# Four edits to the dense part of a four-layer graph network: where ones are counted, where the gate is summed, who adds x, and when fe1 is loaded

## The chip, the cores and the metric

The kernel runs on one core of a Trainium2 chip. The core has a matrix engine (PE), a vector engine (DVE), a scalar engine for activations (ACT), a general engine (GpSimd, POOL in the profile) and a queue for transfers (SP). The metric is the device time of one launch in microseconds, as a median of several runs. A profiled execution is a separate run with a time of its own.

## The reference, cut to what matters

Four layers act on 4096 nodes with 256 features and one adjacency matrix of 4096 x 4096 int32. Each layer normalises x, applies relu, runs a graph block, and adds the result to x. The change concerns the end of layer 0, which has no sum over neighbours left once `h_attn` is known, and the degree of layer 1.

```python
# layer 0, after Wh = h @ W and h_attn = softmax(masked logits) @ Wh
h_enh = silu(_ln(Wh @ fe1_w + fe1_b, fe_ln_g, fe_ln_b)) @ fe2_w + fe2_b
B, C, dt = split(Wh @ W_bcdt + b_bcdt, 3)
hs = Wh * ((softmax(dt + A) * B) @ abp_w + abp_b)
h_part, z = split(hs @ W_hz + b_hz, 2)
hs = (h_part * silu(z) + h_part * D) @ out_w + out_b
hs = hs * (1.0 + C @ cp_w + cp_b)
comb = concatenate([h_attn, hs])
g = sigmoid(silu(_ln(comb @ g1_w + g1_b, g_ln_g, g_ln_b)) @ g2_w + g2_b)
x = x + _ln(g * h_attn + (1.0 - g) * hs + h_enh, ln_g, ln_b)
# layer 1
a = (adj == 1)
deg = sum(a, axis=1)          # needed as 1 / deg for each node
```

## The kernel before, in words

The work is cut into 32 tiles of 128 nodes, and four tiles make a block of 512. The stages follow one another: preparation of layer 0, attention of layer 0, the dense part of layer 0, then layers 1, 2 and 3. A framework schedules the instructions of each engine: it takes the program as Python emits it, works out what depends on what, and fixes an order for each engine and for each transfer queue. Each engine then works strictly through its own order. A tile of a pool with few buffers makes the next user wait for the last reader of the old contents.

The dense part starts after the last attention block. Its weights are loaded at L444 to L455 by transfers that GpSimd issues; their memory is free only once the attention has ended. `dense(b)` (L513) is a generator that handles one block in about 32 steps, and `run_staggered` (L659) starts a new block every 16 steps. So the second half of one block runs beside the first half of the next. Its steps, in order, with the tiles that the prediction names:

- Load x of the block into xt on SP's queue (L517, one buffer), and add ln_b to it on GpSimd (L520). Transpose Wh into whT (copied out of PSUM by ACT for k = 0 and by DVE for k = 1).
- bc (L529 to L552): products with bcw; gain; a softmax over dt with its maximum, exponential, sum and reciprocal, and two multiplications on GpSimd (L545, L548); obc on GpSimd (L550).
- t1 (L555): products with fe1 and the bias fe1_b; `normed` (L471) takes statistics on DVE, rstd on GpSimd, and applies them with four activations on ACT (L481).
- abT (L564): the transposed softmax product, copied out of PSUM by ACT; hsT (L566) from it on DVE.
- `hidden` (L486): transposes of t, then Silu on ACT into zT.
- sz (L576 to L596): 16 pairs of products with W_hz; the first half passes through Silu on ACT and an addition on GpSimd (L586), the second half is multiplied on by DVE (L592).
- henh (L597) and hs (L604): products with fe2 and out_w, summed out of PSUM by DVE (L601, L608).
- comb (L614): transposes of h_attn and hs, copied by ACT and DVE in turn; dh and hs + henh on GpSimd (L622, L623).
- t2 (L625): products with g1, `normed` again, and `hidden` again.
- The gate (L634 to L644): four products with g2, each with its bias added by DVE into f in SBUF (L638), then one tanh of the whole of f on ACT (L642), and two DVE operations on 1024 columns (L643, L644). sigmoid(v) is written as 0.5 + 0.5 tanh(v / 2).
- `normed` of f, times ln_g on GpSimd (L647), and the addition of x, that is xt, on DVE (L648), which writes x of the next layer.

The products take their PSUM tiles from a pool of five buffers (psm), the transposes from one of three (pst).

Beside this runs the counting for layer 1. `with_counts` (L650) takes one step of `count` (L500) after each step of `dense`, so 16 steps for a block, in its first half. A step loads a quarter of an adjacency row tile, 128 x 1024 int32 or 512 KB, into `a` on SP's queue (two buffers), and ACT applies Sign twice, with bias -0.5 and -1.5, and accumulates each along the row into `over` (L507). The difference of the two sums, halved, is the number of ones (L697 to L702). In the profile one such activation is followed by a short instruction that reads the accumulator.

SP's queue carries both the loads of `a` and those of xt, in one order.

Of the kernel before, what the change touches and what calls it, by code (L numbers as in the profile page):

```python
# [21 lines left out]
P = 128  # L22
# [19 lines left out]
def kernel(ctx: ExitStack, tc: tile.TileContext, w: dict, out: bass.AP):  # L42
# [5 lines left out]
    BT = 4  # L48
# [32 lines left out]
    ]  # L81

    counts = ctx.enter_context(ExitStack())
    over_p = counts.enter_context(tc.tile_pool(name="over", bufs=1, side="right"))
    over = over_p.tile([P, NT, 2, NQ], F32, name="over")
    log_wide = const.tile([P, 1], F32, name="log_wide")
# [5 lines left out]
    def load_matrix(pool, name, eng=None):  # L92
        src = w[name]
        k, m = src.shape[0] // P, src.shape[1]
        t = pool.tile([P, k, m], F32, name=f"w_{name}")
        (eng or nc.gpsimd).dma_start(out=t, in_=src.rearrange("(k p) m -> p k m", p=P))
        return t
# [221 lines left out]
    with ExitStack() as l0:  # L319
# [5 lines left out]
        bcw = w_early.tile([P, KD, 2 * S + 1], F32, name="bcw")  # L325
        bcb = w_early.tile([P, 2 * S + 1], F32, name="bcb")
        with ExitStack() as es:
            def finish0(t, acc, rden):
# [35 lines left out]
            with ExitStack() as ps_:  # L364
# [23 lines left out]
                run_staggered([block0(b) for b in range(NB)], 2)  # L388


                bcdt = w["L0_gnn_W_bcdt"].rearrange("(k p) m -> p k m", p=P)
# [35 lines left out]
        with ExitStack() as es:  # L427
# [15 lines left out]

            fe1, fe1_b = load_matrix(wp, "L0_gnn_fe1_w"), row("fe1_b")  # L444
            abp, abp_b = load_matrix(wp, "L0_gnn_abp_w"), column("abp_b")
# [10 lines left out]

            def wide(t):

                return t.rearrange("p (o f) -> p o f", o=1).broadcast_to([P, BT, t.shape[1]])

# [39 lines left out]
            def count(t):  # L500

                for q in range(NQ):
                    a = code_p.tile([P, QW], I32, tag="a", name="a")
                    nc.sync.dma_start(out=a, in_=adj[ts(t, P), ts(q, QW)])
                    for v in range(2):
                        sign = code_p.tile([P, QW], BF16, tag="sign", name="sign", bufs=1)
                        nc.scalar.activation(  # L507
                            sign, a, AF.Sign, bias=limits[:, v : v + 1],
                            accum_out=over[:, t, v, q : q + 1],
                        )  # L510
                    yield

            def dense(b):  # L513
# [118 lines left out]
                yield  # L632
                g1T = yield from hidden(t2, g_g, g_b)
                f = d.tile([P, BT, D], F32, tag="henh", name="f")  # L634
                for i in range(BT):
                    ps = psm.tile([P, D], F32, tag="mm", name="mm")
                    products(ps, lambda k: g1T[:, k, ts(i, P)], lambda k: g2[:, k, :], KI)
                    nc.vector.tensor_tensor(f[:, i, :], ps, g2_b, ALU.add)  # L638
                    if i % 2:
                        yield  # L640

                nc.scalar.activation(f, f, AF.Tanh, scale=0.5)  # L642
                nc.vector.scalar_tensor_tensor(f, f, 1.0, dh, ALU.add, ALU.mult)  # L643
                nc.vector.scalar_tensor_tensor(f, f, 0.5, hs, ALU.mult, ALU.add)  # L644
                yield
                yield from normed(f, "ol")
                nc.gpsimd.tensor_tensor(f, f, wide(ln_g), ALU.mult)  # L647
                nc.vector.tensor_tensor(ha, f, xt, ALU.add)  # L648

# [14 lines left out]
    with ExitStack() as es:  # L664
# [35 lines left out]
        nc.vector.tensor_tensor(rdeg, sums[:, :, 0], sums[:, :, 1], ALU.subtract)  # L700
        nc.vector.tensor_scalar(rdeg, rdeg, 0.5, None, ALU.mult)
        nc.vector.reciprocal(rdeg, rdeg)  # L702
# [308 lines left out]
```

## Time and profile before

| what | value |
|---|---|
| median of 3 runs | 3105.68 us (3105.03 to 3110.4) |
| profiled execution | 3108.19 us, its span 3106.4 us |
| PE, DVE, ACT, POOL busy | 93%, 59%, 41%, 28% of the span |
| attention of layer 0 | about 115 to 632 us |
| dense part of layer 0 | 632 to 1276 us |
| layer 1 | to about 1564 us |
| layers 2 and 3 | to 2133 and 3106 us |

The span is the time between the first and the last instruction of the profiled execution. Busy is the time in which an engine worked on an instruction. PE is pipelined, so its busy time isn't the same as work at its full rate: the granted clock (PEclk, 1.00 is full) says how fast it was allowed to run. An idle time in brackets is that of the engine just before the instruction, with the instruction or transfer that ended it behind the arrow. A line number is that of the kernel before.

### The profile page before, as it was taken

How to read it: one execution, taken by the hardware profiler on the slowest of the kernel's cores; microseconds unless marked ns; L12 is line 12 of the kernel's file. 1: busy time of each engine (PE TensorE's matmuls, PEld its weight loads, DVE VectorE, ACT ScalarE, POOL GpSimd, SP SyncE). 2: the span in 40 equal slices, each digit the busy share in tenths (PEclk: the TensorE clock that was granted, in tenths of full speed). 3: DMA queues.
4: the chain of work that ended last, by engine and by line, in shares of the span. 5: the costliest groups of instructions: out<-in, count | busy, mean ns of one | idle time of the engine just before them, and what ended most of it. 6: DMA issues, size and time to landing. Idle time of an engine off the chain costs nothing.

```text
span 3106.4 us, 34931 instructions
## 1 busy us (share of the span) xinstructions
PE 2881.5 (93%) x13344; PEld 2343.0 (75%) x13344; DVE 1847.5 (59%) x3322; ACT 1282.5 (41%) x1980; POOL 870.1 (28%) x604
## 2 busy tenths in 40 slices
PE   5799999979999999699968999899999999999999
PEld 4688888845555565588857887788888888888888
DVE  5767667324444444544479877755866656656653
ACT  5556655368888884400044443444111211211211
POOL 3556665533232332100016555562000000000000
PEclk9899999989999999899989999999999999999999
DMA  8666664054444441234222221202111111111100
GB/s 209 143 130 137 132 132 106 7 186 129 130 128 127 124 135 37 87 118 140 95 103 80 85 78 69 75 8 68 57 38 33 60 38 33 60 38 33 60 8 7
DMA packets 103128, 268.75 MB, mean 87 GB/s; under 512 B 10704, under 2 KB 24272, under 8 KB 94768
## 3 DMA queue, kind: packets, MB, share of 16 engines
q1 hardware_dynamic: 79104, 220.30, 21.3%
q0 software_dynamic: 22464, 45.51, 8.6%
q8 instruction: 104, 1.70, 0.2%
q10 hardware_dynamic: 1392, 0.72, 0.1%
q14 instruction: 64, 0.52, 0.1%
HBM read 262.22 MB, written 37.81 MB: 97 GB/s over the span
## 4 chain that ended last, share of the span: by engine, by line
PE 34%; issue 28%; ACT 11%; DMA 10%; DVE 10%; POOL 6%; POOLq 0%; ACTq 0%; SPq 0%; DVEq 0%
PE acc L306 16%; PE acc L717 8%; DMA a<-in_adj_dram 6%; PE mm L150 5%; ACT sign L507 5%; POOL y L269 4%; DVE run L229 3%; PE s L150 3%; DVE y L265 2%; PE acc L943 2%; DMA turned<-codesT 1%; DMA ab_row<-l_ab_d 1%; ACT zT L492 1%; ACT t L481 1%; ACT y L295 1%
## 5 line engine op out<-in xcount | busy, mean ns | idle before, releaser
L306 PE MATMUL acc<-v,y 128*128 128x257 f32 x4096 | 930.1, 386 | 52.9 <-ACT hp L742 27.8
L306 PEld LDWEIGHTS acc<-v,y 128*128 128x128 f32 x4096 | 777.2, 192 | 168.3 <-ACT hp L742 32.2
L269 POOL TENSOR_TENSOR y<-y,turned 128x1024 f32<-128x1024 f32 x256 | 544.0, 2137 | 323.1 <-DVE y L265 272.6
L295 ACT ACTIVATE y<-y,sdst 128x512 f32<-128x512 f32 x512 | 343.1, 715 | 359.7 <-POOL y L269 359.7
L265 DVE SCALAR_TENSOR_TENSOR y<-ab_row,cdst,b 128x512 f32<-128x512 f32 x512 | 361.4, 742 | 175.8 <-PE acc L306 110.1
L943 PE MATMUL acc<-v,y 128*128 128x257 f32 x2048 | 454.5, 380 | 0.4 <-DVE rden L951 0.4
L150 PE MATMUL s<-qT,hT 128*128 128x256 f32 x2048 | 445.2, 379 | 0.7 <-ACT qT L891 0.7
L150 PEld LDWEIGHTS s<-qT,hT 128*128 128x128 f32 x2048 | 389.0, 190 | 54.2 <-ACT qT L891 1.4
L943 PEld LDWEIGHTS acc<-v,y 128*128 128x128 f32 x2048 | 387.1, 190 | 55.9 <-issue 0.8
L936 ACT ACTIVATE y<-y 128x1024 f32<-128x1024 f32 x128 | 132.2, 1055 | 714.3 <-DVE y L935 710.0
L229 DVE SCALAR_TENSOR_TENSOR run<-turned,sd,run 128x512 f32<-128x512 bf16 x496 | 373.2, 752 | 68.1 <-DMA turned<-codesT 45.4
L507 ACT ACTIVATE sign<-a,limits 128x1024 bf16<-128x1024 int32 x256 | 294.0, 1148 | 85.4 <-DMA a<-in_adj_dram 81.2
L956 POOL DMA_DIRECT2D out_dram<-o x32 | 17.4, 542 | 934.9 <-DVE rden L951 932.0
L717 PE MATMUL acc<-v,eq 128*128 128x512 f32 x1024 | 240.3, 396 | 0.0
L905 DVE SCALAR_TENSOR_TENSOR y<-code,s 128x512 f32<-128x512 bf16 x256 | 175.8, 687 | 100.9 <-PE s L150 100.6
L717 PEld LDWEIGHTS acc<-v,eq 128*128 128x128 f32 x1024 | 191.9, 188 | 46.6 <-DVE eq L713 0.3
L935 DVE TENSOR_TENSOR y<-y,top 128x1024 f32<-128x1024 f32 x128 | 146.2, 1214 | 43.0 <-PE top L929 43.0
L912 DVE TENSOR_TENSOR mx<-mx,y 128x512 f32<-128x512 f32 x224 | 154.8, 691 | 7.5
L352 ACT ACTIVATE turned<-cT,log_wide 128x1024 bf16<-128x1024 bf16 x128 | 141.6, 1106 | 33.6 <-PE cT L348 33.3
L713 DVE TENSOR_SCALAR eq<-code 128x4096 fp32r<-128x4096 bf16 x32 | 73.4, 2294 | 115.8 <-PE acc L717 115.8
L150 PE MATMUL mm<-hsT,w_L_gnn_W_hz 128*128 128x512 f32 x256 | 118.3, 601 | 1.7 <-DVE hsT L570 1.7
L348 PE MATMUL cT<-identb,adj_t 128*128 128x128 bf16 x1024 | 83.2, 226 | 36.6 <-DVE identb L67 18.6
(219 smaller groups left out, 2742.8 us busy)
## 6 DMA issues: line engine op xcount, KB each, us to landing
a<-in_adj_dram SPq DMA_DIRECT2D x128, 512.0 KB, 3.7
adj_t<-in_adj_dram POOLq DMA_DIRECT2D x128, 256.0 KB, 4.5
codesT<-turned SPq DMA_DIRECT2D x32, 1024.0 KB, 5.2
code<-codesT SPq DMA_DIRECT2D x128, 256.0 KB, 3.8
turned<-codesT SPq DMA_DIRECT2D x32, 1024.0 KB, 4.9
code<-codesT SPq DMA_DIRECT2D x64, 512.0 KB, 4.8
ab_row<-l_ab_d SPq DMA_DIRECT2D x16, 512.0 KB, 3.8
xs<-in_x_dram SPq DMA_DIRECT2D x8, 512.0 KB, 12.2
```

Of the source, the lines that this page charges most:

```text
L150: nc.tensor.matmul(out=ps, lhsT=lhsT_of(k), rhs=rhs_of(k), start=(k == 0), stop=(k == n - 1))
L229: nc.vector.scalar_tensor_tensor(st["run"], code, self.sd[:, j, 1:2], st["run"], ALU.subtract, ALU.min)
L265: nc.vector.scalar_tensor_tensor(y[:, :, k, :], st["ab"][:, 0, :, :], self.cdst[:, c + k : c + k + 1], st["b"], ALU.add, ALU.max,)
L269: nc.gpsimd.tensor_tensor(y, y, mask[:, :, c % QT : c % QT + 2, :], ALU.subtract)
L295: nc.scalar.activation(y[:, :, k, :], y[:, :, k, :], AF.Exp, bias=self.sdst[:, c + k : c + k + 1],)
L306: nc.tensor.matmul(out=accs[b][r], lhsT=y[:, r, k, :], rhs=self.v[:, c + k, :], start=(c + k == 0), stop=(c + k == NT - 1),)
L507: nc.scalar.activation(sign, a, AF.Sign, bias=limits[:, v : v + 1], accum_out=over[:, t, v, q : q + 1],)
L717: nc.tensor.matmul(out=acc, lhsT=eq[:, ts(c, P)], rhs=v1[:, c, :, :], start=(c == 0), stop=(c == NT - 1),)
L905: nc.vector.scalar_tensor_tensor(y[:, :, c : c + 2, :], st["code"][:, :, c : c + 2, :], -BIG / UNIT, ps, ALU.mult, ALU.add,)
L912: nc.vector.tensor_tensor(mx, mx, y[:, :, c : c + 2, :], ALU.max)
L935: nc.vector.tensor_tensor(part, part, top, ALU.subtract)
L943: nc.tensor.matmul(out=accs[r], lhsT=st["y"][:, r, c, :], rhs=v3[:, c, :], start=(c == 0), stop=(c == NT - 1),)
```

## The change

Four edits:

- Counting: of the four quarters of a row, DVE counts the first two. It compares with 1.0 and accumulates the result along the row into a new tile `ones_in`, one operation for a quarter. ACT counts the last two as before, with two signs each. The sums are put together before the reciprocal. Since a step of `count` takes the quarters in order over the four tiles of a block, DVE has the first eight steps of a block and ACT the last eight.
- The gate: two products with g2 share a PSUM tile of 128 x 2 x 256. The bias, the tanh and the first of the two last sums are written back to PSUM, and the second sum writes f in SBUF. All work on 512 columns at a time.
- The addition of x at the end of a block is issued on GpSimd.
- fe1 and its bias have a place in the memory that lives through the attention, and are loaded by SP during the preparation of layer 0, after the loads of x.

```diff
+    HQ = NQ // 2
-    over = over_p.tile([P, NT, 2, NQ], F32, name="over")
+    ones_in = over_p.tile([P, NT, HQ], F32, name="ones_in")
+    over = over_p.tile([P, NT, 2, HQ], F32, name="over")
...
+        fe1 = w_early.tile([P, KD, DI], F32, name="fe1")
+        fe1_b = w_early.tile([P, DI], F32, name="fe1_b")
...
                 run_staggered([block0(b) for b in range(NB)], 2)

+                nc.sync.dma_start(
+                    out=fe1, in_=w["L0_gnn_fe1_w"].rearrange("(k p) m -> p k m", p=P)
+                )
+                nc.sync.dma_start(out=fe1_b, in_=w["L0_gnn_fe1_b"].partition_broadcast(P))
...
-            fe1, fe1_b = load_matrix(wp, "L0_gnn_fe1_w"), row("fe1_b")
...
-            def wide(t):
+            def wide(t, n=BT):
...
-                return t.rearrange("p (o f) -> p o f", o=1).broadcast_to([P, BT, t.shape[1]])
+                return t.rearrange("p (o f) -> p o f", o=1).broadcast_to([P, n, t.shape[1]])
...
                     nc.sync.dma_start(out=a, in_=adj[ts(t, P), ts(q, QW)])
-                    for v in range(2):
+                    if q < HQ:
+                        one = code_p.tile([P, QW], BF16, tag="one", name="one", bufs=1)
+                        nc.vector.tensor_scalar(
+                            one, a, 1.0, 0.0, ALU.is_equal, ALU.add,
+                            accum_out=ones_in[:, t, q : q + 1],
+                        )
+                    for v in range(2 if q >= HQ else 0):
                         sign = code_p.tile([P, QW], BF16, tag="sign", name="sign", bufs=1)
                         nc.scalar.activation(
                             sign, a, AF.Sign, bias=limits[:, v : v + 1],
-                            accum_out=over[:, t, v, q : q + 1],
+                            accum_out=over[:, t, v, q - HQ : q - HQ + 1],
                         )
...
                 f = d.tile([P, BT, D], F32, tag="henh", name="f")
-                for i in range(BT):
-                    ps = psm.tile([P, D], F32, tag="mm", name="mm")
-                    products(ps, lambda k: g1T[:, k, ts(i, P)], lambda k: g2[:, k, :], KI)
-                    nc.vector.tensor_tensor(f[:, i, :], ps, g2_b, ALU.add)
-                    if i % 2:
-                        yield
-
-                nc.scalar.activation(f, f, AF.Tanh, scale=0.5)
-                nc.vector.scalar_tensor_tensor(f, f, 1.0, dh, ALU.add, ALU.mult)
-                nc.vector.scalar_tensor_tensor(f, f, 0.5, hs, ALU.mult, ALU.add)
-                yield
+                for i in range(0, BT, 2):
+                    ps = psm.tile([P, 2, D], F32, tag="mm", name="mm")
+                    for u in range(2):
+                        products(
+                            ps[:, u, :], lambda k: g1T[:, k, ts(i + u, P)],
+                            lambda k: g2[:, k, :], KI,
+                        )
+                    nc.vector.tensor_tensor(ps, ps, wide(g2_b, 2), ALU.add)
+                    nc.scalar.activation(ps, ps, AF.Tanh, scale=0.5)
+                    pair = slice(i, i + 2)
+                    nc.vector.scalar_tensor_tensor(ps, ps, 1.0, dh[:, pair, :], ALU.add, ALU.mult)
+                    nc.vector.scalar_tensor_tensor(
+                        f[:, pair, :], ps, 0.5, hs[:, pair, :], ALU.mult, ALU.add
+                    )
+                    yield
                 yield from normed(f, "ol")
                 nc.gpsimd.tensor_tensor(f, f, wide(ln_g), ALU.mult)
-                nc.vector.tensor_tensor(ha, f, xt, ALU.add)
+                nc.gpsimd.tensor_tensor(ha, f, xt, ALU.add)
...
-        nc.vector.tensor_scalar(rdeg, rdeg, 0.5, None, ALU.mult)
+        counted = vp.tile([P, NT], F32, name="counted")
+        nc.vector.tensor_reduce(counted, ones_in, AX.X, ALU.add)
+        nc.vector.scalar_tensor_tensor(rdeg, rdeg, 0.5, counted, ALU.mult, ALU.add)
         nc.vector.reciprocal(rdeg, rdeg)
```

In the changed kernel the two sums of the gate are at L660 and L661, the compare is at L515, the addition of x at L667.

## The prediction

> **What bounds the kernel now.** I read the page first (PE busy 93% of the span), then the windows by stage, because the change lies in the dense part, 632 to 1276 us. In one stretch of it, by the columns of the first line:
>
> ```profile
> core 0: us, PE busy (x) PEld busy (x) DVE busy (x) ACT busy (x) POOL busy (x), PEclk, DMA share, GB/s
> 840.00:910.00 70.00, 64.01 (x227) 38.98 (x226) 30.88 (x59) 59.71 (x95) 21.96 (x13) 0.95 0.41 124
> ```
>
> PE and ACT are both nearly full, DVE is not. The PE timeline of one period (row groups with their idle time in brackets) shows where PE stood:
>
> ```profile
> 845.36 7.13 PE L150 MATMUL mm<-w_L_gnn_out_w,sz 128*128 128x256 f32 x24 [3.14 <-DVE henh L601]
> ...
> 883.51 3.23 PE L150 MATMUL mm<-abT,w_L_gnn_abp_w 128*128 128x512 f32 x4 [2.85 <-ACT abT L466]
> ```
>
> Windows of 3.82 us over that period show that the granted clock falls after each of the two gaps (the column after POOL):
>
> ```profile
> 844.62:848.44 3.82, 3.08 (x10) 2.58 (x11) 2.20 (x6) 2.48 (x4) 0.00 (x0) 0.75 0.71 222
> 848.44:852.26 3.82, 3.82 (x15) 3.18 (x15) 0.57 (x2) 2.14 (x3) 2.35 (x1) 0.80 0.65 216
> ...
> 882.82:886.64 3.82, 3.13 (x5) 1.30 (x6) 0.75 (x1) 3.79 (x7) 0.00 (x0) 0.67 0.60 195
> 886.64:890.46 3.82, 3.82 (x15) 2.01 (x14) 0.75 (x1) 2.39 (x5) 0.00 (x0) 0.89 0.00 0
> ```
>
> PE's own work per block, from starts in the timeline: 84 records of 512 columns at 0.429 us (8 in 3.43), 96 of 256 at 0.216, 16 of 257 at 0.218, 60 transposes at 0.109: 36.0 + 20.7 + 3.5 + 6.5 = 66.7 us. L647 starts at 764.87, 840.81, 917.17, 995.63, 1071.34, 1146.97 and 1220.12, so a period is 75.9 us. The loss in this one: 6.0 idle and 3.82 x (0.25 + 0.20 + 0.33 + 0.11) = 3.4 of clock, 1.7 per gap; 76.4 - 9.4 is 67.0, so nothing else is lost. Over six periods 6 x 9.2 = 55 us can be had.
>
> The first gap comes from DVE's order: the add of x stands ahead of the sums that free PSUM, and waits for GpSimd.
>
> ```profile
> 919.56 1.22 DVE L648 TENSOR_TENSOR xs<-f,xt 128x1024 f32<-128x1024 f32 x1 [4.58 <-POOL f L647]
> 920.89 1.42 DVE L601 TENSOR_TENSOR henh<-mm,b_L_gnn_fe_b 128x256 f32<-128x256 f32 x4
> ```
>
> The second comes from ACT: signs of the counting stand ahead of the copy of abT.
>
> ```profile
> 880.47 1.15 ACT L507 ACTIVATE sign<-a,limits 128x1024 bf16<-128x1024 int32 x1
> ...
> 882.89 0.56 ACT L466 COPY abT<-tp 128x512 f32<-128x512 f32 x1
> ```
>
> The waits of 630 to 1240 us (total, times, longest) show the counting held up by its loads, and how often both gaps come:
>
> ```profile
> ACT sign L507 <- DMA a<-in_adj_dram: 81.2, 67, 5.1
> ...
> DVE xs L648 <- POOL f L647: 32.3, 7, 4.8
> ...
> PE mm L150 <- DVE henh L601: 17.7, 7, 3.1
> ...
> PE mm L150 <- ACT abT L466: 12.7, 7, 2.9
> ```
>
> and SP's own waits, that the load of xt sits in SP's queue until x is added, with the loads of a behind it:
>
> ```profile
> SPq L517 <- DVE xs L648: 62.7, 7, 37.2
> ```
>
> Prices, by shape (mean ns before the bar, idle after it):
>
> ```profile
> L644 DVE SCALAR_TENSOR_TENSOR f<-f,hs 128x1024 f32<-128x1024 f32 x7 | 17.4, 2480 | 0.0
> L647 POOL TENSOR_TENSOR f<-f,b_L_gnn_ln_g 128x1024 f32<-128x1024 f32 x7 | 16.5, 2351 | 17.0 <-ACT f L481 17.0
> ...
> L643 DVE SCALAR_TENSOR_TENSOR f<-f,dh 128x1024 f32<-128x1024 f32 x7 | 8.6, 1225 | 9.7 <-ACT f L642 9.7
> ```
>
> **What the Trainium skill says.** "TensorE: Matmul & The Clock Gate", Part 1: the clock is halved after an idle window and comes back after sustained work. The trace agrees in kind (0.67 to 0.80 after the gaps). "SBUF — State Buffer", "two separate sides": a GpSimd operation and a DVE operation with two SBUF inputs exclude each other for whole instructions. The trace agrees: L644 takes 2480 ns beside GpSimd's obc, its like L643 1225. "Perfetto Trace Analysis", "Per-engine timelines": DVE and ACT run strictly in order; both orders above agree.
>
> **The change, part by part.**
>
> *Counting.* Per block ACT loses 16 signs at 1.28 us from start to start (845.64 to 846.92 in its timeline), 20.5 of its 64.4 per period. DVE gets 8 operations on 1024 int32. No row shows one. The perf-mode table of "VectorE: DVE Perf Modes" gives an fp32 tensor_scalar in SBUF double rate; L713 runs 4096 in 2294 ns, so 0.7 us is the low end; 1225 (L643's rate, 1024 elements) plus a read of the accumulator (83 ns where L196 does one) is the high one. I take 1.25: 10 us on a DVE that had 34.7, off the path as work. Its waits are not. In the built order ACT has 2, 2, 0, 3, 2, 0, 0 signs between t and abT in blocks 1 to 7. Before there were two or three in each; the seven gaps were 12.7 us (2.1, 1.1, 2.9, 2.1, 2.7, 1.3, 0.5), and I charge five of them the 1.7 of clock: 21.2. Now four stay, at about 1.9 + 1.7, since the signs left are paced by their loads as before: 14.4. Gain 6.8; ends 0 and 21.
>
> *Gate in PSUM.* DVE: 4 x 0.425 + 1.225 + 2.48 = 5.4 becomes 2 x 0.69 + 4 x 0.74 = 4.3; ACT's one tanh of 1.04 becomes two of about 0.6. The last gate product ended at 903.5 and L644 at 909.8. Now 0.69, 0.6, 0.74 and 0.74 with one sz sum between end near 907.6. Two of five PSUM buffers stay taken for some 4 us; PE needs the fifth next one 5 x 1.7 = 8.6 us later, so that is hidden; if the chain waits for DVE's counts, PE waits by what exceeds 8.6. L661 reads PSUM and one SBUF tensor, so obc on GpSimd should no longer stop it.
>
> *x on GpSimd.* DVE loses 1.225 and the wait; GpSimd gets 2.36 more (L647's row) in 23 of 76. Behind it in GpSimd's queue stand xt, dh, hs and bc; bc ended at 867.8 and PE read it at 879.2, so 11 us cover them. While it runs it could stop a count of DVE if that runs at double rate: 0 to 2.4 us a block, and I take 0, since the counts are late anyway. Following the order of the changed program from 907.6: sums and statistics to 910.4, rstd 911.5, ACT 914.0, L647 916.4, x added 918.9, against 920.8. The gap behind henh goes: seven, 17.7 us, with 6.0 of waits for whT just after (2.70, 0.35, 0.35, 1.66, 0.98 in PE's timeline) and 7 x 1.7 of clock: 35.6.
>
> *What is late next* is the load of a behind xt. In the built order xt stands after 37, 59, 80, 102 and 126 loads of a, 16 to a block, DVE's eight first. So the 38th and 103rd (DVE, between two sums of hs), the 81st (the same) and the 60th (ACT, ahead of whT) wait for x added: 918.9, 0.5 of SP, 4.75 to land (921.28 to 926.03 in the trace): 924.1. DVE's count ends 925.4; the last of the cluster waits for a load issued then (3.75): 930.4; whT 931.1. Queued behind are hs, whT and comb; PE, out of buffers of transposes at 925.6, waits 5.5 and loses 1.7: 7.2. Twice that, 8.2 for the 81st (one count more ahead of comb), and on ACT 4.6 + 1.7 = 6.3: 28.9. Blocks 4, 7 and the tail have none. Gain 35.6 - 28.9 = 6.7. Ends: these waits cost nothing if the loads land in time, and 57 or more if every block has one of 8 us.
>
> *First block.* PE stood 3.4 for fe1, 9.9 for bc, 8.4 for t. The eight counts stand ahead of fe_off, with loads of up to 8 us beside the weights; they end near 661, t at 664.2 instead of 668.6: 4.3 won. Between hs sums of this block stands the 17th count, whose buffer waits for ACT's 15th: some 3 + 1.7 lost. Net 0, ends -5 and +5.
>
> *fe1.* Two triggers leave GpSimd's queue (0.76 and 0.56 us), two join SP's after x. 0.77 MB at 230 GB/s is 3.3 us, beside a DMA share of 0.79 between 20 and 60 us: I take 1 us lost, ends 0 and 3.4.
>
> *Tail.* The gate ends 1.3 earlier, the add of x 1.1 later; the two more operations for rdeg are under 0.5 on DVE. Nothing.
>
> Sum: -6.8 - 6.7 + 1 = -12.5. The profiled execution took 3108.2 (span 3106.4 and 1.8 around it), so 3095.7; the median lies 2.5 lower: 3093.
>
> **The rivals.**
> - *PE alone bounds.* Loads land in time, all gaps go: 6 x (75.9 - 67.2) = 52, 3.7 at the tail (its gap of 1.97 and clock), 4 in the first block: 3105.7 - 59.7 = 3046. For it: ACT falls to 44 of 67, and 16 loads at 2.5 to 3.2 us make 45. Against it: xt in SP's queue.
> - *Slower: DVE's counts hold up PSUM.* With two buffers a count comes every (3.7 + 1.25) / 2 = 2.5 us, eight in a row 20 us, and sums run only between. It decides at hs, whT and bc: the gaps of before are 35.6 + 21.2 = 56.8, so above 8.1 us in each of seven blocks it is a loss; at 10 it is 70 against 56.8: 3119. For it: the clusters in the order. Against it: PE needs 14 us for henh and hs anyway, and DVE idled there.
> - *The gap only moves*: as long behind DVE's counts as behind the add of x: 3105.
>
> **Chances.** Forecast 0.46 (own range 3078 to 3099), PE alone 0.22, slower 0.18, moved 0.14. About 0.2% (6 us) is what a measurement can tell from no change: faster 0.68, same 0.14, slower 0.18. Leaving out the outer halves of PE alone and of slower (0.11 and 0.09), the range is 3046 to 3119.
>
> **What would show it.** Periods of L647 near 74 where xt stands inside DVE's cluster, near 68 around block 4; PE's gap before its first out_w products gone; waits of DVE's count for a of some 4 us; L661 near 740 ns; SP waiting for GpSimd at xt. Wrong if no PE gap names whT or hs behind a count, or if gaps appear in every block.

## The result and the profile after

The changed kernel took 3120.88 us (median of 6 runs, 3117.21 to 3126.41) against 3106.26 for the kernel before on the same chip. The ratio is 1.0043 with an interval of 1.0033 to 1.0054: it is slower, by about 14 us (0.4%, and the interval excludes 1), where 12.5 us less were predicted. The profiled execution took 3118.18 us, its span 3116.4, 10.0 more than before.

The starts of the multiplication by ln_g (L666 now, one for each of the eight blocks) give the periods: 770.85, 854.05, 933.79, 1013.57, 1096.16, 1167.46, 1235.52 and 1286.62 us. Before they began at 764.87 and ended at 1272.53. So the first block comes 6.0 later, the next four periods are 83.2, 79.7, 79.8 and 82.6 (before 75.9, 76.4, 78.5 and 75.7), the last three are 71.3, 68.1 and 51.1 (before 75.6, 73.2 and 52.4). The dense part is 14.1 us longer. One stretch of it, by the same columns as in the prediction (the column before the DMA share is the granted clock):

```profile
core 0: us, PE busy (x) PEld busy (x) DVE busy (x) ACT busy (x) POOL busy (x), PEclk, DMA share, GB/s
854.00:924.00 70.00, 59.77 (x210) 36.00 (x209) 35.14 (x74) 43.47 (x69) 22.39 (x13) 0.95 0.45 140
```

ACT is relieved as meant (43.5 of 70 us, 59.7 before) and PE still does less: 59.8 where it did 64.0. The waits of 630 to 1240 us, total, times and longest, say where PE stands now:

```profile
ACT sign L521 <- DMA a<-in_adj_dram: 77.0, 31, 15.6
...
DVE one L515 <- DMA a<-in_adj_dram: 61.7, 39, 4.5
...
DVE henh L615 <- POOL xs L667: 29.9, 6, 7.3
...
PE tp L473 <- DVE whT L477: 14.4, 4, 5.8
...
PE mm L153 <- DVE henh L615: 11.5, 5, 4.1
...
PE mm L153 <- ACT abT L474: 7.6, 4, 3.4
...
PE tp L473 <- ACT whT L474: 6.1, 3, 2.2
```

The gap behind henh has shrunk and not gone (17.7 to 11.5). The waits for copies of whT have grown from 6.0 to 20.5. DVE now waits 61.7 us for a, and SP still waits for the addition of x at the load of xt:

```profile
SPq L531 <- POOL xs L667: 81.2, 6, 59.9
```

Three stretches show how it happens. In the second block DVE's order holds counts between the sums of hs, and the count behind the load of xt waits for its a (start, duration, engine and line, operation, tiles and shapes, in brackets the idle time before and what ended it):

```profile
782.74 1.22 DVE L515 TENSOR_SCALAR_CACHE_REDUCE one<-a 128x1024 bf16<-128x1024 int32 x1 [2.99 <-DMA a<-in_adj_dram]
...
787.74 1.22 DVE L515 TENSOR_SCALAR_CACHE_REDUCE one<-a 128x1024 bf16<-128x1024 int32 x1 [1.28 <-DMA a<-in_adj_dram]
788.88 0.08 DVE L515 DVE_READ_ACCUMULATOR one<-a 128x1 f32 x1
788.88 0.69 DVE L477 COPY whT<-tp 128x512 f32<-128x512 f32 x1
```

PE, out of buffers for transposes, waits for that copy:

```profile
789.63 1.97 PE L473 MATMUL tp<-ident,hs 128*128 128x128 f32 x8 [5.84 <-DVE whT L477]
```

Half a block later counts stand inside the gate's own chain (L657, the tanh on ACT, L660, L661). The tanh of the first pair ended at 833.3, and the sum that needs it starts at 837.17:

```profile
832.00 0.70 DVE L657 TENSOR_TENSOR mm<-mm,b_L_gnn_g_b 128x512 f32<-128x512 f32 x1
836.02 1.22 DVE L515 TENSOR_SCALAR_CACHE_REDUCE one<-a 128x1024 bf16<-128x1024 int32 x1 [3.33 <-DMA a<-in_adj_dram]
837.17 0.08 DVE L515 DVE_READ_ACCUMULATOR one<-a 128x1 f32 x1
837.17 0.69 DVE L660 SCALAR_TENSOR_TENSOR mm<-mm,dh 128x512 f32<-128x512 f32 x1
...
842.16 0.69 DVE L657 TENSOR_TENSOR mm<-mm,b_L_gnn_g_b 128x512 f32<-128x512 f32 x1
843.81 1.22 DVE L515 TENSOR_SCALAR_CACHE_REDUCE one<-a 128x1024 bf16<-128x1024 int32 x1 [0.96 <-DMA a<-in_adj_dram]
```

In the fifth block no count stands inside that chain, but six stand in a row ahead of its first sum, from 1064.39 us on, and five of them wait 1.4 to 1.8 us for their loads. The products of that sum had ended at 1074.62:

```profile
1078.60 1.22 DVE L515 TENSOR_SCALAR_CACHE_REDUCE one<-a 128x1024 bf16<-128x1024 int32 x1 [1.76 <-DMA a<-in_adj_dram]
...
1079.75 0.70 DVE L657 TENSOR_TENSOR mm<-mm,b_L_gnn_g_b 128x512 f32<-128x512 f32 x1
```

In both cases f is late, x is added late, and henh's first sum in the next block waits for it, though the addition is no longer in DVE's queue. PE stood 4.08 us behind the one and 3.70 behind the other, the two longest of its five gaps there. Of the first:

```profile
858.85 1.42 DVE L615 TENSOR_TENSOR henh<-mm,b_L_gnn_fe_b 128x256 f32<-128x256 f32 x4 [6.66 <-POOL xs L667]
```

The prices, by shape, of the new operations:

```profile
L515 DVE TENSOR_SCALAR_CACHE_REDUCE one<-a 128x1024 bf16<-128x1024 int32 x64 | 77.9, 1217 | 62.1 <-DMA a<-in_adj_dram 61.7
...
L667 POOL TENSOR_TENSOR xs<-f,xt 128x1024 f32<-128x1024 f32 x8 | 18.8, 2344 | 0.6
...
L661 DVE SCALAR_TENSOR_TENSOR f<-mm,hs 128x512 f32<-128x512 f32 x16 | 11.0, 688 | 0.4
```

### The profile page after: what moved, and what is told of

Its sections match the earlier page's. It is cut to its first block, busy times and chain, and to the rows that moved or that the text cites. A ratio compares the mean times of both kernels' runs of the same rounds, so it can differ in the third digit from the quotient of the medians.

```text
span 3116.4 us, 34802 instructions
## 1 busy us (share of the span) xinstructions
PE 2875.7 (92%) x13344; PEld 2343.0 (75%) x13344; DVE 1902.0 (61%) x3443; ACT 1130.8 (36%) x1732; POOL 887.5 (28%) x610
## 3 DMA queue, kind: packets, MB, share of 16 engines
q1 hardware_dynamic: 79520, 221.08, 21.2%
## 4 chain that ended last, share of the span: by engine, by line
PE 46%; DVE 5%; issue 4%; POOL 2%; DMA 2%; ACT 1%; POOLq 0%; DVEq 0%; ACTq 0%
PE s L153 13%; PE acc L964 12%; PE acc L309 9%; PE acc L738 7%; PE mm L153 2%; DVE run L232 2%; POOL y L272 1%; DVE y L268 1%; DMA turned<-codesT 1%; PE q_ps L153 1%; POOL pl_rs L119 1%; DVE pl_st L124 0%; ACT y L298 0%; DVE hT L112 0%; PE top L950 0%
## 5 line engine op out<-in xcount | busy, mean ns | idle before, releaser
L738 PE MATMUL acc<-v,eq 128*128 128x512 f32 x1024 | 233.6, 390 | 0.0
L521 ACT ACTIVATE sign<-a,limits 128x1024 bf16<-128x1024 int32 x128 | 146.9, 1148 | 79.3 <-DMA a<-in_adj_dram 77.0
L357 ACT ACTIVATE turned<-cT,log_wide 128x1024 bf16<-128x1024 bf16 x128 | 141.7, 1107 | 34.7 <-PE cT L353 34.4
L515 DVE TENSOR_SCALAR_CACHE_REDUCE one<-a 128x1024 bf16<-128x1024 int32 x64 | 77.9, 1217 | 62.1 <-DMA a<-in_adj_dram 61.7
```

The costliest lines, as they stand in the source:

```text
L521: nc.scalar.activation(sign, a, AF.Sign, bias=limits[:, v : v + 1], accum_out=over[:, t, v, q - HQ : q - HQ + 1],)
L738: nc.tensor.matmul(out=acc, lhsT=eq[:, ts(c, P)], rhs=v1[:, c, :, :], start=(c == 0), stop=(c == NT - 1),)
```

## The experiments

Three theories were on record. A: DVE's counts hold up DVE's sums and copies, and PE behind them. B: the addition of x, slower on GpSimd, holds up henh, because f of one block and henh of the next share one buffer (both tiles have the tag henh). C: the gate keeps PSUM buffers longer. All ratios are to the kernel before, run on the same chip in the same job; 0.001 is 3.1 us. The expectations call ACT ScalarE, DVE VectorE, PE TensorE and SP SyncE. Two cautions hold for all of them. The framework plans each engine's order from estimated durations, so an edit of one instruction can also move others. And a trace is one execution, up to some 10 us off the median of its kernel (only_fe1: 3110.65 us, median 3101.44), so small differences of waits between two traces say little.

### Each edit alone

The four kernels each take one part of the diff above and leave the rest as before: the counting, the gate, the addition of x, the load of fe1.

> The kernel before with the counting edit alone. Theory A (DVE's counts wait for their loads in DVE's order and hold up the sums and copies behind them): slower, 8 to 20 us, with new gaps of PE before transposes that wait for whT. Theory B (the loss comes from the addition of x on GpSimd, which henh waits for because f and henh share one buffer): within 4 us of before, or a few us faster by the lighter ACT. Theory C (the gate's PSUM buffers held longer): as before or faster.

```diff
-                    for v in range(2):
+                    if q < HQ:
+                        one = code_p.tile([P, QW], BF16, tag="one", name="one", bufs=1)
...
+                    for v in range(2 if q >= HQ else 0):
```

Measured: 1.0115 (1.0102 to 1.0128), some 36 us longer. PE's wait behind henh grew to 28.8 us, by the waits of 630 to 1240 us:

```profile
PE mm L152 <- DVE henh L609: 28.8, 6, 6.4
```

The counting alone is by far the costliest edit. Here henh waits for the old, longer gate, and counts lengthen that as well: from the gate's first bias sum to the multiplication by ln_g, by the timelines, it took 21.2 us on average in the first seven blocks of the kernel before and 23.2 here, 25.7 and 25.3 in the two blocks with five counts in the chain.

> The kernel before with the gate edit alone. Theories A and B: faster, 5 to 15 us, because x is added some 2 us sooner in each of seven blocks and henh waits for that. Theory C: slower by 5 us or more, with PE waiting for sums of the gate.

```diff
-                nc.scalar.activation(f, f, AF.Tanh, scale=0.5)
...
+                    nc.scalar.activation(ps, ps, AF.Tanh, scale=0.5)
```

Measured: 0.9977 (0.9966 to 0.9989), a gain of 7 us. The same chain fell from 21.2 to 16.1 us and the gap behind henh vanished. What is late next is ACT's copy of whT, with signs that wait for an a ahead of it:

```profile
PE tp L465 <- ACT whT L466: 21.5, 6, 5.3
```

Theory C is out for the gate alone; all_but_x below bears on it beside the counts.

> The kernel before with only the addition of x moved to GpSimd. Theory B: slower by 7 to 12 us, the wait of henh for the addition longer by 1.1 us in each of seven blocks, and PE's gap before the products with out_w still there. Theory A: the same sign but small, 0 to 5 us. The forecast's own step said that this gap goes: 10 us or more faster.

```diff
-                nc.vector.tensor_tensor(ha, f, xt, ALU.add)
+                nc.gpsimd.tensor_tensor(ha, f, xt, ALU.add)
```

Measured: 1.0038 (1.0023 to 1.0052), 12 us slower. The waits:

```profile
DVE henh L601 <- POOL xs L648: 48.9, 7, 7.0
...
PE mm L150 <- DVE henh L601: 24.9, 7, 4.1
```

With the addition off DVE, henh's sum waits for it all the same, and PE's gap is longer (24.9 for 17.7). It was never DVE's order alone: the shared buffer ties henh to the last reader of f.

> The kernel before with only fe1 and its bias loaded early. All theories: within 4 us of before; at the start 0 to 3.4 us lost to the loads, in the first block up to 4 us won. If it alone loses more than 6 us, all of A, B and C miss a part of the loss.

```diff
+        fe1 = w_early.tile([P, KD, DI], F32, name="fe1")
...
-            fe1, fe1_b = load_matrix(wp, "L0_gnn_fe1_w"), row("fe1_b")
```

Measured: 0.9996 (0.9987 to 1.0005), no difference. In the first block PE waited 3.4 us for fe1 and 9.8 for bc before. With the early load it waits 13.6 for bc (13.5 in the whole change): one wait took the place of the other.

The single edits add to 39 us, the whole change cost 14. They overlap, so the next runs take one edit out of the whole. (The gate and fe1 were not taken out alone.)

### The whole change but one edit

> The whole change with the counting of the ones left as it was before (both halves on ScalarE by two signs); gate in PSUM, x added on GpSimd and fe1 early remain. Theory A (VectorE's counts stand in VectorE's queue and wait for the loads of a, and hold up sums and copies that TensorE waits for): the loss of the whole change goes with them. The alone-runs of the three remaining edits (0.9977, 1.0038, 0.9996) multiply to 1.0011, so about 3107 us against a before of about 3104. Theory B (the addition of x, slower on GpSimd, holds up the first sum of henh, which shares one buffer with f): a loss of 12 us stays of which the gate gives back 7, so 3107 too, but the wait of VectorE for the addition of x stays at about 45 us in all over seven blocks, and TensorE's wait for henh at about 20 us. If the edits interact (the single edits sum to +39 us and the whole change is +15), then either the gate helps more where x is on GpSimd, and this run lies near 3095, or it is the counts that cost less beside the gate, and this run lies near 3107 and the counts' share here is 14 us, not 37.

```diff
-                    if q < HQ:
...
-                    for v in range(2 if q >= HQ else 0):
+                    for v in range(2):
```

Measured: 1.0003 (0.9995 to 1.0011). Without the counts on DVE the loss is gone, and PE's wait behind henh is 2.4 us although x is added on GpSimd. So the counts cost 1.0043 less 1.0003, some 12 us, beside the three other edits. In the dense part they cost more, 17.1 us by the last multiplication by ln_g (1286.62 against 1269.55); layer 1, which is 6.7 us shorter with split counting (last section), hides a part. The gate's chain, from its first bias sum to the multiplication by ln_g, is 15.8 us long on average in the first seven blocks here and 17.2 in the whole change, both well under the 21.2 before. That the counts fill up slack which the gate made would explain why they cost less beside it than alone; no run tests this by itself.

> The whole change with the addition of x left on VectorE. Theory B: the 1.1 us by which GpSimd's addition is longer, seven times, with what it sets off, is taken back: 3109 us by the alone-run of x (+12), with TensorE's wait for henh back near the 18 us of the kernel before. Theory A: the counts still hold up VectorE, so the time stays above the kernel before by 5 us or more (gate -7 and counts +37 would give 3134 if they simply add; 3109 if the whole change's interaction lies between counts and gate). If it is slower than the whole change (over 3120), the move of x to GpSimd pays off beside the counts, and theory B has the sign wrong in the whole.

```diff
-                nc.gpsimd.tensor_tensor(ha, f, xt, ALU.add)
+                nc.vector.tensor_tensor(ha, f, xt, ALU.add)
```

Measured: 1.0048 (1.0036 to 1.0060), the same as the whole change. Beside DVE's counts of this form the move of x costs nothing. Without the counts it costs some 8 us: from about 0.9977 with the gate alone to 1.0003 in all_but_count (an estimate across runs). Against only_count (1.0115) the same run shows what the gate and fe1 are worth beside the counts: some 21 us, where alone they won 7. So theory C is out there too.

### Taking away a wait

> The whole change, but the gated sum f is written over hs and not into the buffer that henh of the next block takes. Henh's first sum then waits for nothing of the block before. Theory B (the buffer shared by f and henh carries the wait): VectorE's wait for the addition of x ahead of henh, 36 us in seven blocks, goes, TensorE's wait for henh, 11.5 us, goes too, and the time falls by 10 to 30 us, to 3091 to 3111, unless hs's own first sum, some 14 us later in the block, takes the wait over (then it is under 1 us per block). The prediction's reading (VectorE's order, x ahead of henh's sums) expects nothing, since x isn't in VectorE's queue any more: 3120. Theory A alone: little, 3115 to 3120, for the counts behind the load of x still hold up VectorE.

```diff
-                f = d.tile([P, BT, D], F32, tag="henh", name="f")
...
-                        f[:, pair, :], ps, 0.5, hs[:, pair, :], ALU.mult, ALU.add
+                        hs[:, pair, :], ps, 0.5, hs[:, pair, :], ALU.mult, ALU.add
...
+                f = hs
                 yield from normed(f, "ol")
```

Measured: 1.0059 (1.0047 to 1.0071), no faster than the whole change. DVE's wait at henh and PE's behind it are both gone from the trace, which shows that the shared buffer made them; but PE now waits as long for whT:

```profile
PE tp L473 <- DVE whT L477: 19.1, 4, 6.9
PE tp L473 <- ACT whT L474: 14.3, 3, 7.7
```

Together 33.4 us, against 20.5 + 11.5 = 32.0 for whT and henh in the whole change. Theory B's wait is real and not what bounds here. A buffer of its own for f, a second one for xt and a third for a were not tried.

> The whole change with the load of x issued from GpSimd's queue and not SyncE's. In SyncE's queue the load of x waits for the addition of x of the block before, 149 us in seven blocks, and the loads of a behind it wait with it; VectorE's count for those a's then waits up to 3 us, and TensorE up to 5.8 us behind whT's copies. Theory A: with the loads of a free of it, VectorE's wait for a (62 us) falls to about 40, ScalarE's (77 us) to about 40, TensorE's waits for whT's copies (14.4 us) go, and the time falls by 10 to 25 us, to 3096 to 3111. Theory B alone: henh still waits for the addition of x, so no change, 3117 to 3121.

```diff
-                nc.sync.dma_start(
+                nc.gpsimd.dma_start(
                     out=xt, in_=x[ts(b, BW), :].rearrange("(t p) d -> p t d", p=P)
```

Measured: 1.0038 (1.0026 to 1.0050), at most some 2 us better and not told apart from the whole change. The wait behind whT at 790 us stayed (6.76 for 5.84): with SP free of xt, two of the counts there still wait 3.12 and 1.82 us for their loads of a. The blocked queue is not the cause by itself.

### The form of the counting

> The whole change with the halves of the counting split by row tile, even tiles on VectorE and odd tiles on ScalarE, and not by column quarter. The loads of a come in the order of the four tiles of a block in turn, so with the split by quarter eight counts in a row fall to VectorE and then eight to ScalarE; split by tile they take turns. Theory A, sharpened: the trace shows that in a row of eight VectorE takes 1.3 us per count but gets an a only every 2.5 to 5 us (two buffers, 3.7 us from issue to landing), so it waits 1 to 3 us at each, and the sums and copies of the dense part behind it wait too. With turns VectorE has two landings' time per count: its wait for a, 62 us before the second layer, falls below 25, TensorE's 14.4 us behind VectorE's copies of whT go below 5, and the time is 3100 to 3110. If what costs is the 1.3 us of each count in VectorE's queue, whatever it waits for: 3116 to 3122. ScalarE then waits for a at its own turns, which may take part of the gain.

```diff
-                    if q < HQ:
+                    if t % 2 == 0:
...
-                    for v in range(2 if q >= HQ else 0):
+                    for v in range(2 if t % 2 else 0):
```

Measured: 1.0051 (1.0039 to 1.0063). Turns bring nothing: DVE's wait for a rose from 61.7 to 87.9 us, three counts now stand in the gate's chain of each of five blocks, and PE's waits for whT grew from 20.5 to 32.0. The time (3120) is the one expected if the counts' own work in DVE's queue costs:

```profile
PE tp L473 <- DVE whT L477: 17.1, 6, 4.5
PE tp L473 <- ACT whT L474: 14.9, 5, 3.4
...
PE mm L153 <- DVE henh L615: 8.7, 5, 2.8
```

> As the run with alternating counts, with the addition of x left on VectorE, too. Theory B: 3 to 9 us faster than the alternating counts with x on GpSimd, since the first sum of henh waits 1.1 us less in each block. If henh's wait is hidden by the waits for a (as the whole change with x on VectorE says, 3119 against 3121): no difference between the two.

The edit is that of alternate and of all_but_x together.

Measured: 1.0007 (0.9999 to 1.0015), 14 us better than with x on GpSimd and more than either expectation had. PE's waits for whT fell from 32.0 to 17.2:

```profile
PE tp L473 <- DVE whT L477: 9.9, 6, 4.6
PE tp L473 <- ACT whT L474: 7.3, 5, 2.3
PE mm L153 <- DVE henh L615: 1.8, 3, 1.0
```

So the move of x costs 14 us here, 8 to 12 where ACT counts, and nothing beside the counts of the change. On GpSimd the addition takes 2.34 us against 1.22, and henh and the load of xt wait for it. Whether that wait is the last to end seems to depend on the counts; no run tests it further.

> The whole change with a loaded in pieces of 512 columns into four buffers, in the same SBUF, in place of 1024 into two; every count and sign then covers 512 columns, and there are twice as many (complete computation). If two buffers of a set the pace (the next load can't be issued before a count has ended), four smaller ones let three loads be on the way while one is counted: VectorE's wait for a, 62 us, falls below 40 and the time to 3105 to 3113. If VectorE's own work sets the loss, it grows by the fixed part of 64 more counts (some 0.15 us each, 10 us in all): 3120 to 3128.

```diff
-            code_p = es.enter_context(tc.tile_pool(name="l0_code", bufs=2))
+            code_p = es.enter_context(tc.tile_pool(name="l0_code", bufs=4))
...
-                    a = code_p.tile([P, QW], I32, tag="a", name="a")
+                    a = code_p.tile([P, CW], I32, tag="a", name="a")
```

Measured: 1.0025 (1.0018 to 1.0033), 5 to 6 us better than the whole change, in the range expected if the buffers set the pace, with DVE's wait for a at 40.6 us (below 40 was expected). A count now blocks DVE for 0.68 us and two more loads can be on their way. The sum of the counts' work is a little larger, 87.0 us against 77.9, so it isn't the sum that costs. The pace of the buffers, or the size of the piece for which DVE is held, makes a part of the loss, 5.6 of the 12 to 14 us; the run doesn't part the two.

### Work or waiting

> The whole change, but VectorE's 64 counts read a tile of weights that has long been in SBUF in place of a (so the number of ones is not computed; the loads of a and ScalarE's half stay). It keeps the instructions and their time in VectorE's queue and takes their waits away. Theory A as waiting: VectorE's 62 us of waits for a are gone, TensorE's wait for whT's copies by VectorE goes, 3098 to 3108. Theory A as work: the 83 us of counting in VectorE's order cost what they cost, 3115 to 3121. The wait of henh for the addition of x is in both the same, 36 us or more.

```diff
-                            one, a, 1.0, 0.0, ALU.is_equal, ALU.add,
+                            one, fe2.rearrange("p k d -> p (k d)"), 1.0, 0.0, ALU.is_equal, ALU.add,
```

Measured: 1.0058 (1.0046 to 1.0070). It does not answer: with their operand there after one wait of 6.4 us for its load, all 64 counts were ordered into the first block (the last at 743 us), which came 13 us later than in the whole change. PE stood 11.44 us at one copy of whT behind a row of them.

> The whole change, VectorE's 64 counts reading the tile of fe1's weights, which lies in SBUF before the dense part begins, in place of a (so the number of ones is not computed; the loads of a and ScalarE's half stay). It is the run resident without its flaw: there the first counts waited 6.4 us for the load of fe2, TensorE stood 11.4 us for it, and the first block alone came 13 us late, while the next four periods took 314.4 us against 325.3 in the whole change and 308.7 in the one without VectorE's counts. If waiting for a is what costs (theory A as waiting), some 10 to 13 us of the 15 that the counts cost go: 3106 to 3111. If the counts' own 1.3 us each in VectorE's queue cost: 3116 to 3121.

```diff
-                            one, a, 1.0, 0.0, ALU.is_equal, ALU.add,
+                            one, fe1.rearrange("p k d -> p (k d)"), 1.0, 0.0, ALU.is_equal, ALU.add,
```

Measured: 1.0040 (1.0028 to 1.0052). The time is in the range of work, but the run isn't what it was meant to be. Again all 64 counts were ordered into the first block (the last at 734 us), and PE stood 11.44 us at the same copy, so the late load was not the flaw of the run before. The block ends 13.4 us later than without counts (784.4 against 771.0), and the later periods are close to those of no_ones. It shows only that 64 counts in one block, without waits, cost 13 us there. Work without waits in the places of the whole change was not measured.

> The whole change with VectorE's 64 counts left out (the ones of that half are not counted; the loads of a and ScalarE's half stay). What it gains on the whole change is all that the counts cost, as work and as waiting; what it gains on resident_fe1 is their work. Theory A as waiting: within 5 us of resident_fe1, 3101 to 3108. As work: 10 us or more below resident_fe1. If ScalarE's 64 signs fewer help, it may fall below the run without the edit of counting (3106), to 3085 to 3095: then the loss is not from what was taken from ScalarE.

```diff
+    nc.vector.memset(ones_in, 0.0)
...
-                    if q < HQ:
-                        one = code_p.tile([P, QW], BF16, tag="one", name="one", bufs=1)
...
```

Measured: 1.0005 (0.9998 to 1.0013). The time of the counts is gone, 12 us, and the time is that of all counting on ACT (1.0003): relieving ACT of half of its signs won nothing. Two things hide in it. Layer 1 is 6.7 us shorter here than with all counting on ACT, so by the times the dense part is still some 7 us behind that run (an estimate; the single traces, with their last multiplication by ln_g at 1268.57 and 1269.55, don't show it). And PE's idle time from 640 us on is 64.3 us, as in the kernel before (65.0). The gap behind henh is gone, but PE now waits for t, where signs stand ahead of the activations of `normed`:

```profile
PE tp L474 <- ACT t L490: 32.8, 14, 11.9
```

Before, those waits were 13.2 us.

> As no_ones, with the addition of x on VectorE (the ones of one half are not counted). Theory B: with no count in VectorE's queue the first sum of henh is what TensorE waits for, and x on GpSimd costs what it cost in the alternating counts (3120 against 3108) or alone (12 us): 8 to 12 us faster than no_ones. If it is no faster, x on GpSimd costs only where VectorE's counts wait behind it.

The edit is that of no_ones and of all_but_x together.

Measured: 0.9998 (0.9991 to 1.0004), some 2 us less than no_ones, with intervals that overlap, and not the 8 to 12 expected. Where DVE and ACT have both room, x on GpSimd hardly costs.

> The whole change, each of VectorE's 64 counts reading only the first 64 of the 1024 columns of its a (the others of that half are not counted; all loads and ScalarE's half stay). It keeps every wait of VectorE for a load of a, and takes most of the 1.2 us of work of each count away. With VectorE's counts left out altogether the ratio was 1.0005, in the whole change 1.0043. If waiting is what costs (theory A as waiting): ratio 1.0030 to 1.0045, about 3112 to 3118. If the work costs, which delays what stands behind it in VectorE's order and with it the release of a and the sums that TensorE waits for: 1.0000 to 1.0015, 3102 to 3107. In between: both, by that share.

```diff
-                            one, a, 1.0, 0.0, ALU.is_equal, ALU.add,
+                            one[:, 0:64], a[:, 0:64], 1.0, 0.0, ALU.is_equal, ALU.add,
```

Measured: 0.9998 (0.9989 to 1.0006), the whole loss gone, with every count still waiting for its a, and longer in all than in the whole change:

```profile
DVE one L515 <- DMA a<-in_adj_dram: 77.4, 45, 4.7
```

A count took 217 ns for 1217. So waits for a of this sum need not cost anything, and what was taken away is the microsecond of work in each count, which keeps DVE from what stands behind it and gives the buffer of a back later. Which of the two it is stays open, and how much is the order: with the shorter counts the plan put none of them between the gate's steps of the second block, where the whole change has five, and that chain took 15.9 us for 22.0.

### What beats both

> The kernel before with the gate in PSUM and fe1 loaded early, and the load of x issued from GpSimd's queue; counting all on ScalarE, x added on VectorE. With the gate alone (3097) TensorE's gap behind henh was gone, and 21.5 us of gaps behind ScalarE's copies of whT had come up, where ScalarE's signs wait for loads of a that stand behind the load of x in SyncE's queue. If that reading holds, these gaps go and the time is 3080 to 3092. If ScalarE's signs are bound by the pace of the loads anyway, or another wait follows at once: 3095 to 3098. The alone-run of fe1 (no difference) puts nothing to it.

The edits of all_but_count, all_but_x and xt_by_gpsimd together.

Measured: 0.9970 (0.9961 to 0.9979), 3096.08 us, the fastest of all and better than the kernel before and the change. It isn't told apart from the gate alone (0.9977): PE still waits 18.6 us for ACT's copies of whT (21.5 there), and ACT's signs still wait 70.2 us for a (81.5 there). So the load of xt in SP's queue was at most a small part of those waits.

> What the runs point to, together: counting alternating between VectorE and ScalarE by row tile, x added on VectorE, its load issued from GpSimd's queue, f written over hs, the gate in PSUM, fe1 early. Against the alternating counts with x on VectorE (3108): the wait for x in SyncE's queue and that of henh are gone, as in the runs that changed these alone (5 us, and none). Theory A: ScalarE and VectorE wait 146 and 87 us for loads of a there, and as much of it as is due to the load of x goes: 3095 to 3103. If the pace of the two buffers of a sets the waits: 3104 to 3109.

The edits of alternate_x_on_dve, xt_by_gpsimd and f_in_hs together.

Measured: 1.0020 (1.0013 to 1.0028). The remedies together are no better than alternating counts with x on DVE (1.0007). By its expectation the two buffers of a, and not the load of xt, set the waits there; of the other runs only half_tiles bears on that.

## Why the prediction was wrong, point by point

PE's idle time from 640 us to the last multiplication by ln_g, by what ended it, from the timelines:

| idle before, ended by | before | predicted | after |
|---|---|---|---|
| henh | 17.7 | 0 | 11.5 |
| copies of whT, hs behind counts | 6.0 | 22.1 | 20.5 |
| abT | 12.7 | 7.6 | 7.6 |
| t | 13.2 | 13.2 | 17.3 |
| fe1's load, bc | 13.2 | 13.2 | 13.5 |
| sums of sz and hsT | 1.7 | 1.7 | 5.8 |
| all (with smaller ones) | 65.0 | 58.3 | 76.7 |

The column in the middle is what the prediction's terms come to, with the first block left as before. The rest of the time, in which PE worked, was to fall by 6.8 with the clock; it rose from 567.5 to 569.9. 11.7 + 2.4 is the 14.1 of the dense part. Predicted was -6.7 - 6.8 = -13.5.

The miss has two parts. One is a cost that was put at nothing, 12 to 14 us. The other is a gain that doesn't come even where that cost is taken away: no_ones and short_ones are at 1.0005 and 0.9998, not 12.5 us below.

- *"10 us on a DVE that had 34.7, off the path as work"* is the step that failed: it put the work of DVE's counts at nothing. The price was right: 1217 ns and 83 for the read, against 1.25. But taking the counts away (no_ones) returns 12 us, and taking only their work away (short_ones) 14. "Its waits are not" looked for the cost in the wrong place: in short_ones DVE waited longer for a (77.4 us for 61.7), and the time fell. The low end of 0.7 us came from "VectorE: DVE Perf Modes", the perf-mode tier table, which gives an fp32 tensor_scalar in SBUF double rate. The form with an accumulated result ran at 1217 ns for 1024 int32 and at 1215 for 1024 fp32 here (resident_fe1), so it has no such rate here.
- *"The gap behind henh goes"* failed too: 11.5 us stayed. It rested on "The first gap comes from DVE's order". But f and henh share a buffer, so henh waits for the addition of x on whatever engine it is (only_x: 24.9 for 17.7; f_in_hs: gone). And the time at which x is added was worked out from a gate with "one sz sum between", while counts stand in that chain or ahead of it: the second block's took 22.0 us, the seven on average 17.2, where the gate alone has 16.1. Without the counts the gap does go (2.4 in all_but_count, none in no_ones), but its price does not come back: in f_in_hs the waits for whT grew as much, in no_ones those for t. The prediction added up its gaps one by one, and the runs show that they stand in for each other.
- *The clock*: the working time was missed by 9.2. At the prediction's own 1.7 us for a gap, the five gaps behind henh make 8.5 of it, an estimate that no run tests.
- *What is late next* was right in kind and in place. In time the four gaps were 5.84 for 5.5, 2.02 for 4.6, 3.95 for 6.5, and 2.64 + 1.95 for 5.5: the first was met, the others were smaller. The sum of the table comes so near (20.5 for 22.1) partly by luck, for it also holds 1.98 of the first block and 2.18 at 1112 us.
- *Counting on ACT*: four waits for abT at 1.9, 7.6 in all, were expected, and 7.6 in four came (2.11, 1.00, 3.38 and 1.10). That ACT's signs can hold up t instead was not reckoned with: 17.3 for 13.2, and 32.8 in no_ones.
- *Gate in PSUM*: undervalued. The prediction made its chain 2.2 us shorter. Alone it became 5.1 shorter, and the time 7 us. L661 took 688 ns, also where obc ran beside it, as expected.
- *First block, "Net 0"*: held up to 701 us. The transposes of v start at 700.84, at 701.03 before; t was not 4.3 earlier, but 0.6 later (667.13 against 666.56). The 6.0 us by which the block's multiplication by ln_g is later were lost after that: 1.98 of idle at a copy of whT behind a count (3 was put on it), 1.9 in four waits for t of the second block, and a halved clock just after (0.50 from 737.79 to 741.61 us, where the kernel before kept 1.00).
- *fe1*: right, nothing measurable either way.
- *Tail, "Nothing"*: of the 14.1 us, 4.1 came back after the dense part, from layer 1, which the prediction left out (below).

Of the rivals, the slower one (counts hold up PSUM, 3119) came within 2 us of the time, but its mechanism holds only in part. The row of six counts in the fifth block did come at 2.8 us a count, near its 2.5. Yet there was no gap of 10 us in each of seven blocks, but PE's idle time was 10.2, 10.1, 8.1 and 8.8 us in four periods, where it was 6.7, 6.0, 5.0 and 5.6 before, and 0.6 in the sixth, where the counts had ended.

## What to carry to other kernels

When a wait is read off the order of an engine, look also at the buffer that the waiting instruction writes: if its last reader is the same instruction, moving that one to another engine leaves the wait. Work that is moved to an engine "with room" is priced by what stands behind it in that engine's order, in the chain that ends last, and not by the room; before moving it, list the instructions of the built order from well ahead of the first step of that chain to its last. A gap that is closed is a gain only if no other wait stands close behind it: f_in_hs closed the gap behind henh and won nothing. And an edit that shortens the chain that bounds, as the gate did, is worth trying by itself before it is bundled with others that lengthen it.

## What was not expected of the hardware

- The clock fell after a single gap of 2 us. "TensorE: Matmul & The Clock Gate", Part 1, ties the halving to an idle window of about 3.4 us. In the kernel before, 24 products with out_w took 7.13 us after a gap of 1.97, with no other gap in the 30 us ahead of it, and in the 3.41 us from 1225.43 on the granted clock was 0.50 (the column before the DMA share):

```profile
1224.32 7.13 PE L150 MATMUL mm<-w_L_gnn_out_w,sz 128*128 128x256 f32 x24 [1.97 <-DVE henh L601]
```

```profile
1225.43:1228.84 3.41, 3.41 (x10) 2.70 (x9) 0.70 (x2) 0.00 (x0) 1.16 (x1) 0.50 0.40 135
```

Not every gap of 2 us does it: in the run xt_by_gpsimd the same 24 products took 5.45 us after one of 2.12.

- Layer 1, which no edit touches, got faster. Its products with eq, in the same 1024 instructions, took (busy, mean ns) in the whole change and in the kernel before:

```profile
L738 PE MATMUL acc<-v,eq 128*128 128x512 f32 x1024 | 233.6, 390 | 0.0
```

```profile
L717 PE MATMUL acc<-v,eq 128*128 128x512 f32 x1024 | 240.3, 396 | 0.0
```

In all fourteen traces with split counting, no_ones among them, it is 233.5 or 233.6 us, and in the six with all counting on ACT 239.3 to 240.3, at a granted clock of 1.00 in both. These 6 to 7 us hide a part of what the change costs in the dense part. Why is not settled; a different place of tiles in SBUF is only a guess, and no run tried it.
